# Split edge searches, a division moved to VectorE, and seven-product forms for layer 0's neighbour sums and two chunks of the second v projection

## The chip, the cores and the metric

One NeuronCore of a Trainium2 chip. The time is the device time of one execution of the whole kernel, in microseconds (us); a lower number is better. TensorE is also called PE (its weight loads PEld), VectorE DVE, ScalarE ACT, GpSimd POOL and SyncE SP. All arrays are f32.

## The reference

A graph network over N = 384 nodes and 12672 edges, in two blocks with a residual and a normalisation before each. First 16-head attention of width 1024 under a mask that is built from the edges; then a relational graph convolution of two layers (width 768, R = 6 relations, B = 4 bases).

```python
h = relu(layernorm(x))
q, k, v = h @ wq.T + bq, h @ wk.T + bk, h @ wv.T + bv
q2, k2, v2 = q @ wiq.T + biq, k @ wik.T + bik, v @ wiv.T + biv      # 16 heads of 64
mask[src, dst] = softplus(w)[type5 - 1]        # -inf elsewhere, the diagonal always set
x = x + (softmax(q2 k2' / 8 + mask) v2) @ wo.T + bo

h = relu(layernorm(x)); y = relu(h @ w_in + b_in)
for l in 0, 1:
    W[r] = sum_b comp[l, r, b] * basis[l, b]
    agg[dst] += (y @ W[r])[src] / count[r, dst]     # every edge, by its relation r
    y = batchnorm(relu(agg + y @ root[l] + bias[l]) + y)
x = x + layernorm(y @ w_out + b_out)
```

## The kernel before

Nodes lie in three chunks of P = 128 (NT = 3), features in chunks of 128 too (KD = 8 for 1024, KC = 6 for 768). The orders of PE, DVE, POOL and SP, and after q of ACT, are those in which the code calls them: each engine runs its instructions in that order, and a waiting one holds back all behind it.

**Seven products.** A product of two matrices cut in 2 x 2 blocks is made with seven block products instead of eight. Sums of blocks are formed on DVE ahead of it (`output_sums` of weights, `node_sum` of nodes, in attention; `weight_sums`, `last_sums`, `node_sums` in the convolution); `multiply` or `times` runs one block product; ACT copies results out of PSUM and DVE adds others to them. A bank (of eight in PSUM) is used again in the same part, so PE waits there for the copy or addition that reads it. In attention, q2, k, k2 and v are made so, in four parts each (`plan`, 16 parts), with `rest` as the product that one part leaves to the next.

**Edges.** `edge_steps` is a generator; `fill(1)` advances it by one step in each part. It finds, for every edge, whether others fall in the same cell. `find_cells(p)` loads a piece of keys (SP), shifts them (DVE), runs one search for the mask (`find(0, ...)`: one DVE operation per 128 edges, 9 or 12 in most pieces) and returns the second search, that for the counts. In pieces from step 3 on both are called in the same step. POOL then scatters with indirect DMAs: `put_mask` (L261) into four mask tables and `put_count` (L266) into two count tables `atab`. The last `fill(1000)` issues what is left: the remaining counts on POOL, and on DVE the operations that merge the four mask tables into `mask8` (L308 to L315).

**Second v projection.** `second_v(half, t, w)` makes 512 columns of v2 for node chunk t with 8 matmuls of 512. Four of them run after v, the other two between the first scores (`scores`, `exponents`, `normalise` of the softmax).

**Counts.** When the scatters are done, SP and POOL load the tables into A (one [128, 3, 384] slice for each relation; the second table is added by the DMA). `add_up(r)` sums the slice over its three chunks on POOL; `share(r)` sums that over partitions with one matmul (ps_cnt), takes the reciprocal on DVE and multiplies A[:, r] by it on POOL; then `mix(l, r, At, bs)` adds comp times A[:, r] into At[:, b] (ACT for r = 0, DVE for the others). A written plan, `between`, puts shares and mixes between PE's matmuls: its key is (layer, basis, chunk), where chunk 4 stands for the end of a basis and basis B for the root product.

**A layer.** For each of four bases, seven products and two chunk rows make H = y @ basis[b] (L846, L840); then y @ root (L880) into six banks `pr`; then the neighbour sums, H' At over bases and node chunks, into the same banks. In layer 0 that is `add_neighbours`, 72 matmuls of 384 columns (L897), features' banks one after the other, with the weight sums of layer 1's first basis put after the third; in layer 1 it is seven products over three pairs of feature chunks (L947), 126 matmuls of 192 columns, whose operands T1..T4 (from At) and feature sums (from H) DVE makes just before.

Of the kernel before, what the change touches and what calls it, by code (L numbers as in the profile page):

```python
# [51 lines left out]
def gnn_kernel(ctx: ExitStack, tc: tile.TileContext, out, x, edges, chunks, cols, rows, small,  # L52
# [120 lines left out]
    def edge_steps(ep, none, zero):  # L173
# [115 lines left out]
        for find_more in rest:  # L289
            find_more()  # L290
        for step in range(2, 18):
            yield
            for i in {5: (0,), 6: (1,), 7: (2, 3), 8: (4, 5)}.get(step, (step - 4,) if 10 <= step < 16 else ()):
                clear(i // R, i % R)
            if step in (3, 6, 8, 10, 12, 14, 16):
                find_cells(max(3, step // 2 + 1))()
            for p in {8: (3,), 9: (4,), 10: (5,), 11: (6,), 16: (7, 8), 17: (9,)}.get(step, ()):
                put_rounds(p)
# [31 lines left out]
    def add_up(r):  # L330
        sums[r] = late.tile([P, N], F32, tag="sum", name="sum", bufs=2)
        nc.gpsimd.tensor_tensor(sums[r], A[:, r, 0, :], A[:, r, 1, :], ALU.add)
        nc.gpsimd.tensor_tensor(sums[r], sums[r], A[:, r, 2, :], ALU.add)

    def share(r):

        ps = next_bank("ps_cnt", ring[1:])
        nc.tensor.matmul(ps[:, :N], ones, sums[r], start=True, stop=True)
        rn = late.tile([P, N], F32, tag="rn", name="rn", bufs=2)
        nc.vector.tensor_scalar(rn, ps[:, :N], 1.0, None, ALU.max)  # L340
        nc.vector.reciprocal(rn, rn)  # L341
        nc.gpsimd.tensor_tensor(A[:, r], A[:, r], rn[:, None, :].to_broadcast([P, NT, N]), ALU.mult)  # L342
        if r + 2 < R:
            add_up(r + 2)


    with ExitStack() as inner:
# [68 lines left out]
        with tc.tile_pool(name="edge", bufs=1, side="right") as ep:  # L416
# [101 lines left out]
            q2, k2, v = made["q2"], made["k2"], made["v"]  # L518
            v2 = ap.tile([P, NT, D], F32, tag="T", name="v2", bufs=4)

            def second_v(half, t, w):
                ps = next_bank("ps_v2", (4, 5, 6, 7))
                for k in range(KD):
                    nc.tensor.matmul(ps, v[:, k, t * P:(t + 1) * P], w[k // 4][:, k % 4, :],  # L524
                                     start=(k == 0), stop=(k == KD - 1))
                return lambda: nc.scalar.copy(v2[:, t, half * 512:(half + 1) * 512], ps)

            for half in range(2):
                w = [wload(wiv[half, j], "w_v2") for j in range(2)]
                for t in range(NT - 2 * half):  # L530
                    second_v(half, t, w)()
# [87 lines left out]
        for f in (0, 2):  # L619
            scores(f)  # L620
            scores(f + 1)
            put_v = second_v(1, f // 2 + 1, w)
# [9 lines left out]
        for g in range(STEPS + 1):  # L632
# [14 lines left out]
            if f + 2 == STEPS:  # L647
# [9 lines left out]
                for r in range(R):  # L657
# [3 lines left out]
                    if 0 < r < 3:  # L661
# [104 lines left out]
    with tc.tile_pool(name="conv", bufs=1) as cp:  # L766
# [41 lines left out]
        def mixes(l, r, *bs):  # L808
            return lambda: mix(l, r, At, bs)

        between = {(0, 1, 1): shares(0), (0, 1, 2): shares(1),
                   (0, 2, 0): lambda: (mix(0, 0, At), share(2)), (0, 2, 1): mixes(0, 1, 0, 1), (0, 2, 2): mixes(0, 1, 2, 3),
                   (0, 2, 4): shares(3),
                   (0, 3, 0): mixes(0, 2, 0, 1), (0, 3, 1): lambda: (mix(0, 2, At, (2, 3)), share(4)),
                   (0, 3, 2): mixes(0, 3, 0, 1), (0, 3, 4): shares(5),
                   (0, 4, 0): mixes(0, 4, 0, 1), (0, 4, 1): mixes(0, 5, 0, 1), (0, 4, 2): mixes(0, 3, 2, 3),
                   (0, 4, 3): mixes(0, 4, 2, 3), (0, 4, 4): mixes(0, 5, 2, 3),
# [10 lines left out]
        for l in range(L):  # L828
# [49 lines left out]
            for k in range(KC):  # L878
                for o in range(KC):
                    nc.tensor.matmul(pr[o], w[k // 2][:, k % 2, o * P:(o + 1) * P], XT[:, k, :], start=(k == 0),  # L880
                                     stop=(k == KC - 1 and l == L - 1))
                if k == 0:
                    rest()
                go_between(l, B, k)
            if l + 1 < L:
                w = load_basis(l + 1, 0)
            else:

                room = late.tile([P, R * NT * N], F32, tag="A", name="room")
                rowsB = room[:, :3 * D].rearrange("p (j d) -> p j d", j=3)  # L890
                for j, r in enumerate((R_BOUT, R_LNG, R_LNB)):
                    nc.scalar.dma_start(rowsB[:, j, :], rows[r:r + 1, :].to_broadcast([P, D]))

            def add_neighbours(o, bs):
                for b in bs:
                    for n in range(NT):
                        nc.tensor.matmul(pr[o], H_[:, b, n, o * P:(o + 1) * P], At[:, b, n, :],  # L897
                                         start=False, stop=(b == B - 1 and n == NT - 1))
# [21 lines left out]
            def begin(o, func=AF.Identity):  # L920

                c = l * KC + o
                nc.scalar.activation(XN[:, o, :], pr[o], func, bias=cols_sb[:, CB + c:CB + c + 1])

            if l + 1 < L:
                for o in range(KC):
                    add_neighbours(o, (0, 1))
                for o in range(KC):
                    add_neighbours(o, (2, 3))
                    begin(o, AF.Relu)  # L930
                    normalise_layer(*measure(o))
                    if o == 2:
                        T = weight_sums(w)
            else:


                def h(o, i):

                    return H_.rearrange("p b n d -> p (b n) d")[:, i * 6:i * 6 + 6, o * P:(o + 1) * P]

                def q(i, j):

                    return At.rearrange("p b n d -> p (b n) d")[:, i * 6:i * 6 + 6, j * HN:(j + 1) * HN]

                def times(ps, x, y, start=False, stop=True):
                    for c in range(6):
                        nc.tensor.matmul(ps, x[:, c], y[:, c], start=start and c == 0, stop=stop and c == 5,  # L947
                                         skip_group_check=True)

                room2 = keep.tile([P, KD * N], F32, tag="hT", name="room2")  # L950
                T1, T2 = [room2[:, i * 1152:(i + 1) * 1152].rearrange("p (c d) -> p c d", c=6) for i in range(2)]
                T4 = keep.tile([P, 6, HN], F32, tag="mask8", name="T4")
                nc.vector.tensor_tensor(T1, q(0, 1), q(0, 0), ALU.subtract)
                nc.vector.tensor_tensor(T2, q(1, 1), T1, ALU.subtract)
                T3 = q(0, 1)
                nc.vector.tensor_tensor(T3, q(1, 1), q(0, 1), ALU.subtract)
                nc.vector.tensor_tensor(T4, q(1, 0), T2, ALU.subtract)
                spaces = [room2[:, 2304:]] + [room[:, 3 * D + i * 768:3 * D + (i + 1) * 768] for i in range(5)]
                spaces = [v.rearrange("p (c o) -> p c o", c=6) for v in spaces]

                def feature_sums(p):

                    s0, s1, s3 = spaces[p % 2 * 3:][:3]
                    o0, o1 = 2 * p, 2 * p + 1
                    S.append((s0, s1, h(o1, 0), s3))
                    for dst, x, y, op in ((s0, h(o1, 0), h(o1, 1), ALU.add), (s1, s0, h(o0, 0), ALU.subtract),
                                          (h(o1, 0), h(o0, 0), h(o1, 0), ALU.subtract),
                                          (s3, h(o0, 1), s1, ALU.subtract)):
                        nc.vector.tensor_tensor(dst, x, y, op)
                        yield  # L970

                S = []
                for _ in feature_sums(0):
                    pass
                pairs = KC // 2

                def take(o, j, ps):
                    dst = XN[:, o, j * HN:(j + 1) * HN]
                    nc.vector.tensor_tensor(dst, dst, ps, ALU.add)

                def rectify(o):
                    nc.scalar.activation(XN[:, o, :], XN[:, o, :], AF.Relu)
                    return o

                def first_of(p):
                    pa = next_bank("ps_c", range(8))[:, :HN]
                    times(pa, h(2 * p, 0), q(0, 0), True)
                    return pa

                pa = first_of(0)  # L990
                for p in range(pairs):
                    times(pr[2 * p][:, :HN], h(2 * p, 1), q(1, 0))
                for o in range(KC):
                    begin(o)
                take(0, 0, pa)
                ready = None
                for p in range(pairs):
                    last = p == pairs - 1
                    sums = iter(()) if last else feature_sums(p + 1)
                    o0, o1 = 2 * p, 2 * p + 1  # L1000
                    pc = next_bank("ps_c")[:, :HN]
                    times(pc, S[p][0], T1, True)
                    take(o1, 1, pc)
                    if ready:
                        normalise_layer(*ready)
                    next(sums, None)
                    times(pa, S[p][1], T2)
                    take(o0, 1, pa)
                    next(sums, None)
                    times(pc, S[p][3], q(1, 1))  # L1010
                    take(o0, 1, pc)
                    ready = measure(rectify(o0))
                    if last:
# [118 lines left out]
```

## Time and profile before

| what | value |
|---|---|
| three runs | 744.85 us median (740.45 to 747.54) |
| the profiled execution's own time | 735.77 us |
| its span, first to last instruction | 734.0 us |
| PE, PEld busy | 713.5, 496.8 us |
| DVE, POOL, ACT busy | 472.9, 323.3, 147.2 us |
| PE clock granted, mean | 0.996 |

The profile is of one execution. Busy time is what an engine's instructions took; the PE column counts two records for each f32 matmul. A row of a group reads: line, engine, operation, output <- inputs, shape, count | busy us, mean ns of one | idle time before them and what ended most of it. In a timeline row, the idle time before an instruction stands in brackets with its releaser. A releaser is inferred; where several were waited for it is the last one seen.

### The profile page before, as it was taken

Reading aid. Unit: us, or ns where it says so; the run is one execution under the profiler, and the core shown is the slowest. Engines: PE = TensorE matmul, PEld = TensorE weight load, DVE = VectorE, ACT = ScalarE, POOL = GpSimd, SP = SyncE. Lnnn points to the kernel's source line nnn. Section 1 sums busy time; section 2 is a strip of 40 time slices with the busy share of each in tenths; the row PEclk is TensorE's granted clock in tenths of the full one; section 3 lists DMA queues with packets and bytes.
Section 4 is the critical chain, followed back from the end, with each engine's and each line's share of the span. In section 5 each row is a group of like instructions: output and inputs, shape, how many; then the busy total and the mean of one; then the engine's idle time right before and its main releaser. Section 6 shows DMA issues by size and latency. Waiting matters only on the chain.

```text
span 734.0 us, 8299 instructions
## 1 busy us (share of the span) xinstructions
PE 713.5 (97%) x3024; PEld 496.8 (68%) x3024; DVE 472.9 (64%) x1228; ACT 147.2 (20%) x338; POOL 323.3 (44%) x242
## 2 busy tenths in 40 slices
PE   8999989999999999999999999899999999999995
PEld 8759989999964444445995555555555555579943
DVE  6895897877504499625424779990187676506756
ACT  3201111111111477510131131100013111001100
POOL 1456777788886788587784454310000000030000
PEclk9999999999999999999999999999999999999999
DMA  7797766743447322623527953321003123700001
GB/s 296 261 346 231 221 182 209 212 148 115 116 119 240 59 1 2 215 0 47 127 2 169 312 163 129 129 83 46 0 1 107 66 85 129 271 29 1 1 29 57
DMA packets 40533, 90.96 MB, mean 124 GB/s; under 512 B 19644, under 2 KB 27680, under 8 KB 36270
## 3 DMA queue, kind: packets, MB, share of 16 engines
q1 hardware_dynamic: 18478, 79.62, 30.9%
q0 software_dynamic: 21008, 8.42, 10.4%
q10 hardware_dynamic: 1008, 2.41, 0.9%
q8 instruction: 23, 0.38, 0.2%
q14 instruction: 16, 0.13, 0.1%
HBM read 79.27 MB, written 11.16 MB: 123 GB/s over the span
## 4 chain that ended last, share of the span: by engine, by line
PE 86%; DVE 11%; ACT 1%; issue 1%; DMA 1%; DVEq 0%; ACTq 0%
PE ps_g L846 13%; PE ps_g L840 10%; PE ps_c L897 6%; PE ps_c L880 6%; PE ps_q L395 6%; PE ps_v L524 6%; PE ps_k L377 6%; PE ps_c L947 6%; PE ps_v L377 5%; PE ps_y L615 5%; PE ps_f L1054 4%; DVE same L250 3%; PE ps_q L377 3%; PE ps_x L377 3%; PE ps_o L608 2%; PE ps_s L563 2%
## 5 line engine op out<-in xcount | busy, mean ns | idle before, releaser
L266 POOL DMA_INDIRECT atab<-count,at x99 | 160.0, 1616 | 50.6 <-DMA atab<-count,at 26.2
L261 POOL DMA_INDIRECT mtab<-m_val,at x99 | 104.1, 1052 | 57.0 <-issue 24.4
L1041 POOL TENSOR_TENSOR x_sb<-x_sb,room 128x1024 f32<-128x1024 f32 x3 | 7.0, 2347 | 158.1 <-DMA room<-in_rows 158.1
L326 DVE SCALAR_TENSOR_TENSOR At<-A,small_sb,At 128x1152 f32<-128x1152 f32 x40 | 62.9, 1635 | 0.0
L840 PE MATMUL ps_g<-T,S 128*128 128x384 f32 x144 | 49.1, 486 | 0.0
L846 PE MATMUL ps_g<-w_c,XT 128*128 128x384 f32 x144 | 48.0, 487 | 0.0
L846 PE MATMUL ps_g<-w_c,XN 128*128 128x384 f32 x144 | 47.6, 486 | 0.0
L897 PE MATMUL ps_c<-At,H 128*128 128x384 f32 x144 | 46.6, 486 | 0.0
L395 PE MATMUL ps_q<-hT,w_q 128*128 128x384 f32 (+1 forms) x160 | 41.8, 422 | 1.4 <-ACT hT L90 1.4
L524 PE MATMUL ps_v<-w_v,v 128*128 128x512 f32 x96 | 41.9, 594 | 0.0
L840 PEld LDWEIGHTS ps_g<-T,S 128*128 128x128 f32 x144 | 27.4, 190 | 19.1
L897 PEld LDWEIGHTS ps_c<-At,H 128*128 128x128 f32 x144 | 27.4, 190 | 19.1
L846 PEld LDWEIGHTS ps_g<-w_c,XN 128*128 128x128 f32 x144 | 27.4, 190 | 19.1
L846 PEld LDWEIGHTS ps_g<-w_c,XT 128*128 128x128 f32 x144 | 27.2, 190 | 19.2 <-DVE H L861 0.6
L395 PEld LDWEIGHTS ps_q<-hT,w_q 128*128 128x128 f32 x160 | 28.5, 190 | 14.1 <-ACT hT L90 1.7
L377 PE MATMUL ps_k<-T,S 128*128 128x192 f32 x192 | 35.8, 330 | 0.0
L615 PE MATMUL ps_y<-w_o,attT 128*128 128x512 f32 x80 | 35.0, 595 | 0.0
L576 DVE CUSTOM_DVE_ANT_0 s<-ps_s,mask 128x384 f32<-128x384 f32 x48 | 24.5, 548 | 15.4 <-PE ps_s L563 15.4
L342 POOL TENSOR_TENSOR A<-A,rn 128x1152 f32<-128x1152 f32 x6 | 19.4, 3236 | 31.7 <-DVE rn L341 31.7
L524 PEld LDWEIGHTS ps_v<-w_v,v 128*128 128x128 f32 x96 | 18.0, 190 | 22.6 <-issue 22.6
L377 PEld LDWEIGHTS ps_k<-T,S 128*128 128x128 f32 x192 | 32.7, 194 | 0.0
L1054 PE MATMUL ps_f<-w_out,XN 128*128 128x512 f32 (+1 forms) x84 | 31.1, 531 | 0.0
(250 smaller groups left out, 1316.6 us busy)
## 6 DMA issues: line engine op xcount, KB each, us to landing
w_c<-in_basis SPq DMA_DIRECT2D x24, 768.0 KB, 6.2
atab<-zero SPq DMA_DIRECT2D x12, 576.0 KB, 8.2
A<-atab POOLq DMA_DIRECT2D x10, 576.0 KB, 9.8
w_c<-in_root SPq DMA_DIRECT2D x6, 768.0 KB, 5.5
w_q<-in_wq SPq DMA_DIRECT2D x4, 1024.0 KB, 11.8
w_q<-in_wiq SPq DMA_DIRECT2D x4, 1024.0 KB, 10.1
w_k<-in_wk SPq DMA_DIRECT2D x4, 1024.0 KB, 7.0
w_k<-in_wik SPq DMA_DIRECT2D x4, 1024.0 KB, 6.2
```

The costliest lines, as they stand in the source:

```text
L261: nc.gpsimd.indirect_dma_start(mtab[c // PER][:, :], bass.IndirectOffsetOnAxis(at[:, 0, c:c + 1], 0), m_val[:, c:c + 1], None)
L266: nc.gpsimd.indirect_dma_start(atab[0 if i < 18 - DEALT else i % 2][:, :], bass.IndirectOffsetOnAxis(at[:, 1, c:c + 1], 0), count[:, 1, c: ...
L326: nc.vector.scalar_tensor_tensor(At[:, b], A[:, r], w, At[:, b], ALU.mult, ALU.add)
L377: nc.tensor.matmul(ps, a[:, k, :], b[:, k, :], start=start and k == 0, stop=(k == 3), skip_group_check=not start)
L395: nc.tensor.matmul(ps[o][:, c], wt_[:, k, o * P:(o + 1) * P], src[:, k, c], start=(k == 0 and c.start == 0), stop=(k == KD - 1 and c.stop ...
L524: nc.tensor.matmul(ps, v[:, k, t * P:(t + 1) * P], w[k // 4][:, k % 4, :], start=(k == 0), stop=(k == KD - 1))
L615: nc.tensor.matmul(ps, attT[:, k, t * P:(t + 1) * P], w_o[half][k // 4][:, k % 4, :], start=(k == 0), stop=(k == KD - 1))
L840: nc.tensor.matmul(ps, x[:, c], y(c), start=start and c == 0, stop=(c == 2), skip_group_check=not start)
L846: nc.tensor.matmul(ps, block(XT, n, i)[:, c], w[c][:, i, o * HC:(o + 1) * HC], start=(first and c == 0), stop=(c == 2 and (i == 1 or ps is ...
L880: nc.tensor.matmul(pr[o], w[k // 2][:, k % 2, o * P:(o + 1) * P], XT[:, k, :], start=(k == 0), stop=(k == KC - 1 and l == L - 1))
L897: nc.tensor.matmul(pr[o], H_[:, b, n, o * P:(o + 1) * P], At[:, b, n, :], start=False, stop=(b == B - 1 and n == NT - 1))
L1054: nc.tensor.matmul(p, XT[:, k, t * P:(t + 1) * P], w[k // 2][:, k % 2, c0:c1], start=(k == 0), stop=(k == KC - 1))
```

## The change

1. *Searches*: from step 3 on, the second search of a piece is called in the step after the first.
2. *Division*: `share` multiplies A[:, r] on DVE; four `sums` tiles instead of two, so that `add_up` of relations 0 to 3 is issued with A's transfers on POOL, and `share(r)` issues that of r + 4. The plan `between` of layer 0 is written anew.
3. *Second v projection*: chunks 0 and 1 are made in seven block products for each half; chunk 2 stays as it was and runs between the first scores.
4. *Layer 0's neighbour sums* take the form that layer 1's had. Its sums lie in other tiles, one of them of the weights' pool.

```diff
         for find_more in rest:
             find_more()
+        rest = []
         for step in range(2, 18):
             yield
+            if rest:
+                rest.pop()()
...
             if step in (3, 6, 8, 10, 12, 14, 16):
-                find_cells(max(3, step // 2 + 1))()
+                rest.append(find_cells(max(3, step // 2 + 1)))
...
-        sums[r] = late.tile([P, N], F32, tag="sum", name="sum", bufs=2)
+        sums[r] = late.tile([P, N], F32, tag="sum", name="sum", bufs=4)
...
-        nc.gpsimd.tensor_tensor(A[:, r], A[:, r], rn[:, None, :].to_broadcast([P, NT, N]), ALU.mult)
-        if r + 2 < R:
-            add_up(r + 2)
+        nc.vector.tensor_tensor(A[:, r], A[:, r], rn[:, None, :].to_broadcast([P, NT, N]), ALU.mult)
+        if r + 4 < R:
+            add_up(r + 4)
...
+            VS = [sum_tile(i).rearrange("p k n -> p (k n)")[:, :512].rearrange("p (k n) -> p k n", k=4)
+                  for i in (1, 2, 3, 4)]
+            for dst, a, b, op in ((VS[0], va(1, 0), va(1, 1), ALU.add), (VS[1], VS[0], va(0, 0), ALU.subtract),
+                                  (VS[2], va(0, 0), va(1, 0), ALU.subtract), (VS[3], va(0, 1), VS[1], ALU.subtract)):
+                nc.vector.tensor_tensor(dst, a, b, op)
...
+                for dst, a, b in ((T1, vb(half, 0, 1), vb(half, 0, 0)), (T2, vb(half, 1, 1), T1),
+                                  (T3, vb(half, 1, 1), vb(half, 0, 1)), (T4, vb(half, 1, 0), T2)):
+                    nc.vector.tensor_tensor(dst, a, b, ALU.subtract)
+                return T1, T2, T3, T4
...
+            VT = [output_weights(half) for half in range(2)]
+            def v_products(half):
+                pa, pb, pc = [ps[:, :256] for ps in vbanks[half]]
+                T1, T2, T3, T4 = VT[half]
+                multiply(pa, va(0, 0), vb(half, 0, 0), True)
+                nc.scalar.copy(v_out(half, 0, 0), pa)
+                yield
+                multiply(pb, va(0, 1), vb(half, 1, 0), True)
+                add_out(half, 0, 0, pb)
+                yield
+                multiply(pc, VS[0], T1, True)
+                nc.scalar.copy(v_out(half, 1, 1), pc)
+                yield
+                multiply(pa, VS[1], T2)
+                nc.scalar.copy(v_out(half, 0, 1), pa)
+                yield
+                multiply(pc, VS[3], vb(half, 1, 1))
+                add_out(half, 0, 1, pc)
+                yield
...
+                multiply(pd, va(1, 1), T4, True)
+                multiply(pa, VS[2], T3)
+                def last():
+                    nc.scalar.copy(v_out(half, 1, 0), pa)
+                    add_out(half, 1, 1, pa)
+                    add_out(half, 1, 0, pd)
+                yield last
+            first, second = v_products(0), v_products(1)
+            for products, n in ((first, 2), (second, 2), (first, 3)):
+                for _ in range(n):
+                    next(products)
+            next(first)()
+            for _ in range(3):
+                next(second)
+            next(second)()
             fill(1000)
...
-            put_v = second_v(1, f // 2 + 1, w)
+            put_v = second_v(f // 2)
...
-                    if 0 < r < 3:
+                    if 0 < r < 5:
                         add_up(r - 1)
...
-        between = {(0, 1, 1): shares(0), (0, 1, 2): shares(1),
-                   (0, 2, 0): lambda: (mix(0, 0, At), share(2)), (0, 2, 1): mixes(0, 1, 0, 1), (0, 2, 2): mixes(0, 1, 2, 3),
-                   (0, 2, 4): shares(3),
-                   (0, 3, 0): mixes(0, 2, 0, 1), (0, 3, 1): lambda: (mix(0, 2, At, (2, 3)), share(4)),
-                   (0, 3, 2): mixes(0, 3, 0, 1), (0, 3, 4): shares(5),
-                   (0, 4, 0): mixes(0, 4, 0, 1), (0, 4, 1): mixes(0, 5, 0, 1), (0, 4, 2): mixes(0, 3, 2, 3),
-                   (0, 4, 3): mixes(0, 4, 2, 3), (0, 4, 4): mixes(0, 5, 2, 3),
+        between = {(0, 1, 0): shares(0), (0, 1, 1): shares(1), (0, 1, 2): lambda: mix(0, 0, At),
+                   (0, 1, 4): mixes(0, 1, 0, 1), (0, 2, 0): shares(2), (0, 2, 2): shares(3),
+                   (0, 2, 4): mixes(0, 2, 0, 1), (0, 3, 0): shares(4), (0, 3, 1): shares(5),
+                   (0, 3, 4): lambda: [mix(0, r, At, (0, 1)) for r in (3, 4, 5)],
+                   **{(0, 4, r): mixes(0, r, 2, 3) for r in range(1, R)},
...
+            room2 = keep.tile([P, KD * N], F32, tag="hT", name="room2")
+            spaces = [room2[:, 2304:]]
             if l + 1 < L:
+                spaces += [v.rearrange("p i k o -> p (i k o)")[:, i * 768:(i + 1) * 768] for v, n in
+                           ((cp.tile([P, 4, 3, P], F32, tag="S", name="sums"), 2),
+                            (wpool.tile([P, 2, 6, P], F32, tag="w", name="sums"), 2)) for i in range(n)]
+                spaces.append(cp.tile([P, 3, HC], F32, tag="T4", name="sums").rearrange("p c d -> p (c d)")[:, :768])
                 w = load_basis(l + 1, 0)
...
-            if l + 1 < L:
-                for o in range(KC):
-                    add_neighbours(o, (0, 1))
-                for o in range(KC):
-                    add_neighbours(o, (2, 3))
-                    begin(o, AF.Relu)
-                    normalise_layer(*measure(o))
-                    if o == 2:
-                        T = weight_sums(w)
-            else:
...
             XT = XN
             if l + 1 < L:
                 S = node_sums(XT)
+                T = weight_sums(w)
```

## The prediction

> **What bounds the kernel now.** I read the page's busy shares, then TensorE's waits by releaser, then its instructions in order of time around each wait. Columns of a waits row: who waited for whom, total us, times, longest. Of a timeline row: start, us, engine, line, tile, shape, count, and what ended the idle time before it.
>
> ```profile
> PE 713.5 (97%) x3024; PEld 496.8 (68%) x3024; DVE 472.9 (64%) x1228; ACT 147.2 (20%) x338; POOL 323.3 (44%) x242
> ```
>
> ```profile
> PE ps_k L377 <- DVE k L502: 4.3, 3, 2.9
> PE ps_c L880 <- DVE H L853: 2.2, 1, 2.2
> PE ps_v L377 <- DVE v L502: 1.1, 1, 1.1
> ```
>
> ```profile
> 101.48 1.46 PE L377 MATMUL ps_k<-T,S 128*128 128x192 f32 x8
> 105.86 2.61 PE L377 MATMUL ps_k<-T,w_k 128*128 128x192 f32 x8 [2.92 <-DVE k L502]
> 108.26 2.14 PE L377 MATMUL ps_k<-T,S 128*128 128x192 f32 x8
> ```
>
> TensorE (PE) is busy 97% of 734.0 us: time goes only with PE work or PE waits. Nearly all waits are on VectorE (DVE), in two places: the searches (L250) and the end of layer 0's last basis.
>
> The chain that ended last, by time, prices the PE work (start, us, what; one f32 matmul leaves two records):
>
> ```profile
> 209.96 27.47 PE ps_v L524 x64
> 348.05 6.91 PE ps_y L687 x32
> 499.77 46.44 PE ps_c L897 x144
> 654.57 40.95 PE ps_c L947 x252
> ```
>
> So 512 columns cost 0.858 us, 256 cost 0.432, 384 cost 0.645 and 192 cost 0.325: width alone counts.
>
> **Split searches.** The 16 parts of q2, k, k2 and v are 7 products of 1.30 us each: 145.6 us. They stand between 55.55 and 209.96, 154.4 us: 8.8 lost. The waits are 5.7 of it (4.3, 1.1, and 0.3 in q2). The 2.92 wait costs more: its two next groups take 4.38 (105.86 to 110.24) instead of 2.60, and the clock over 103 to 112 was 0.81. In a searching part DVE has sums 2.5, key shift 0.95, two searches of 3.7 each, plus adds, against 9.1 us of PE. Split, the part has 7.1 plus adds and the next gets the other 3.7. Tightest is part 0 of q2: T sums end 58.82, S sums 61.35, search 65.05, and the add that frees the bank 65.6; PE wants it at 65.95. I take 8.5 gained. Ends: 5 (small waits come back) and 8.8.
>
> Here a rule is weighed. The Trainium skill, "TensorE: Matmul & The Clock Gate", Part 1 (What's actually happening), puts the drop to half rate after an idle window of some 3.4 us. The idle here is 3.08 (102.78 to 105.86), under a window, so read strictly it costs nothing beyond itself and the edit brings 7.0. The row shows 1.78 more: I take the row. For the new waits below, each under 2 us, the short waits' row holds (after 1.1 us of waiting at 183.70 the group took 0.1 more).
>
> **Second v projection.** Two chunks leave L524: 32 matmuls of 512 (27.47) become 7 products x 4 x 2 halves = 56 of 256, 24.2. Chunk 2 keeps 16 matmuls beside the scores, as before. Gain 3.3. DVE gets 4 sums of 512, 8 of 1024 and 8 adds out of PSUM: about 2.5 + 9.3 + 3. Count from the end of ps_v L377. v is whole at 0.5; the sums of half 0 end at 7.8, half 1 at 12.4; PE wants them from 6.9 (only T1, ready by 4.4) and 15.6: covered. The last add ends at 25.1. *Behind it in DVE's queue stand the mask operations* (L308 to L315), today at 224.1 to 232.6 in idle time. They take 8.5, so the mask is ready at 33.7. PE has done four scores and the 7.07 of second_v at 32.8 and wants banks 0 to 3 again; the exponents free them from 34.1 to 35.6. PE waits 1.7; with restart 1.8. Ends: 0 and 4. Net of this part: 1.5.
>
> **The relation table is the new limit.** Upstream gains make 8.5 + 1.5 = 10.0. But the table comes from POOL's scatters, which do not speed up:
>
> ```profile
> 385.05 1.55 POOL L266 DMA_INDIRECT atab<-count,at  x1 [0.30 <-issue]
> 392.67 1.36 POOL L658 DMA_DIRECT2D A<-atab  x1 [6.07 <-DVE T L795]
> ...
> 404.19 1.01 POOL L332 TENSOR_TENSOR sum<-A 128x384 f32<-128x384 f32 x1
> 405.28 1.60 POOL L333 TENSOR_TENSOR sum<-sum,A 128x384 f32<-128x384 f32 x1
> ```
>
> (I read the 6.07 as the landing of SP's A<-atab, issued at 388.11.) The first two sums stand at 401.1 and 406.9. The counts of relations 0 and 1 move one site earlier: on today's clock to 409.7 and 414.2. Ten us earlier, the second is wanted at 404.2. A scatter stretches beside a DVE operation with two SBUF inputs (2.36 at 200.29, inside L516's 1.22, against 1.55), and v's new sums are such: I add 1.0 to the chain, so sum 1 stands at 407.9. PE waits 3.7 over both; upstream keeps 6.3. Ends: chain 1.3 earlier (POOL's one wait on search results, gone) or 6 later. Upstream losses below 3.7 are thus free. On POOL two add_up pairs are put between the last A transfers. Sum 2 then stands near 414, sum 3 near 422, the last two by 434; they are wanted from 425 on, after the gain.
>
> **Division on DVE, mixes reordered.**
>
> ```profile
> L342 POOL TENSOR_TENSOR A<-A,rn 128x1152 f32<-128x1152 f32 x6 | 19.4, 3236 | 31.7 <-DVE rn L341 31.7
> ...
> 470.65 5.00 DVE L326 SCALAR_TENSOR_TENSOR At<-A,small_sb,At 128x1152 f32<-128x1152 f32 x2
> 555.15 5.39 DVE L326 SCALAR_TENSOR_TENSOR At<-A,small_sb,At 128x1152 f32<-128x1152 f32 x4
> 629.92 1.35 DVE L953 TENSOR_TENSOR room<-At 128x1152 f32<-128x1152 f32 x1
> ```
>
> A mix costs 2.5 beside POOL's division and 1.33 without POOL. The division itself is not in DVE's rows: nearest is L953, 1.35 (broadcast operand unseen; ends 1.3 and POOL's 3.24). The wait of 2.2 at 473.8 goes (PE stood 2.35, its group 0.2 slower): 2.6. Check with t = 0 at the first L846 (PE: basis 19.35 or 22.6 us each): a share is 0.58 + 2.6 + 1.35 = 4.5. DVE does sums 4.4, mixes 2.7, T4 1.5, two shares 9.0, adds 1.4 per basis: 19 in 22.6. ScalarE's first mix (4 x 1.2) stands ahead of its copies, ends as PE's next product runs: no wait. The reordered mixes give the cover back: last H add at 88, then 16 mixes, 21.3, to 109.
>
> **Neighbour sums of layer 0.** 72 matmuls of 384 (46.44) become 126 of 192, exactly L947's 40.95: gain 5.5. The rule that speaks against it: same page, Back-to-back issue gap, says that spacing is set by weight load and matmul both, so narrow matmuls pay more. The weight-load row has 190 ns, two per matmul: 0.38. Were they not hidden, 126 x 0.38 = 47.9, a loss of 1.4. But L947 ran at 0.325 on that very shape, so the loads overlap: 5.5. DVE adds 4 sums of At (5.3) and 4 feature sums (3.5) behind the mixes: At done 109, T1..T4 115, first S 116; PE wants At's second half at 114, S at 121. Cover 5. Per pair the code is the last layer's, where PE never waited. At the end DVE normalises 4.8 after PE's last product (700.3 against 695.5 today), then S 2.1, then weight sums 4.4; before, weight sums lay under L897. PE starts with layer 1's c = 0, which needs features 0 and 1 only, wants S at 11.6 (ready 6.9) and the last T1 at 12.9 (10.4): no wait, 1 to 2 us of cover. If gone: up to 3. SP's next basis loads go past one wpool tile lent to the sums, freed after pair 1, 12 us ahead of need.
>
> **Sum.** 6.3 + 2.6 + 5.5 = 14.4. The profiled span 734.0 becomes 719.6, its time 735.77 becomes 721.4. The median of the runs is 744.85, 9.1 above the profiled execution, so the forecast there is 744.85 - 14.4 = **730.4**.
>
> **Rivals.**
> 1. *Upstream is kept whole.* The chain comes earlier too, no wait for it or the mask: 744.85 - 8.8 - 3.3 - 2.6 - 5.5 = 724.7. For: 40 us of POOL's waits are DMA landings, not fixed. Against: 198 scatters of 1.05 and 1.62 with 0.3 between fill the rest. Chance 0.12.
> 2. *The table comes 6 later.* Sum 1 at 412.9, so upstream keeps 414.2 - 412.9 = 1.3: 744.85 - 1.3 - 8.1 = 735.4. For: scatters stretched beside v's sums, loads colliding with A's transfers. Against: the softmax's DVE work left scatters at 1.55. Chance 0.16.
> 3. *DVE becomes the bound of layer 0.* Division at 3.24 (+11.3 for six), mixes at 2.29 (first four today took 9.16; +19 for twenty), less 15 of cover: 15 late at the first S, 745. For: VectorE's share is over 9 tenths there now. Against: POOL has left but for twelve 1 us adds. Chance 0.06.
> 4. *Slower: the scatter chain takes over.* Each scatter at 2.36 instead of 1.55 delays sum 1 by 0.8, and from 406.9 on every us of it is the end's. Of the site's 7.3 (414.2 - 406.9) and the other parts' 8.1, together 15.4, nineteen stretched scatters leave nothing; thirty come 24 late, 744.85 + 24 - 15.4 = 753.5. Place: the scatters from 210 to 386. Against: the new DVE work there is 15 us, some 8 scatters. Chance 0.04.
>
> Forecast 0.62. A measurement of this kernel can tell about 1%, 7.4 us. Faster by over 1% (below 737.4): forecast, 1 and nearly all of 2, 0.87; within: 3 and the rest, 0.09; slower 0.04. The range reaches from rival 1, less most of the runs' spread (the lowest is 4.4 under the median), to rival 2 and as much of it above: 721 to 739.
>
> **What would show it.** Right: no wait on DVE in ps_q, ps_k, ps_v of over 0.5 and clock 1.00 there; ps_v2 24.2 us; a wait of about 1.7 at a score for the mask chain; waits of together 2 to 5 at ps_cnt, for POOL's sums; none at L880; layer 0's neighbour sums 41 us. Wrong: a gap of over 1 us at the first S product or at the start of layer 1; sum 1 after 414; search waits again over 3.

## The result, and the profile after

| kernel | median us | lowest to highest | runs | against the kernel before |
|---|---|---|---|---|
| before, first runs | 744.5 | 740.45 to 747.54 | 4 | |
| after, first runs | 731.18 | 729.67 to 733.46 | 4 | 0.9855 (0.9808 to 0.9901) |
| before, beside the experiments | 737.7, 737.94, 737.6 | 735.44 to 743.63 | 44, 39, 18 | |
| after again | 731.04 | 727.54 to 736.98 | 13 | 0.9912 (0.9887 to 0.9937) |

The changed kernel takes 731 us, as forecast (730.4). But the forecast was 14.4 us under a median of 744.85, and 101 later runs of the kernel before, on three chips, have medians near 737.7. The first four runs of before lay high; beside 18 of its runs the changed kernel is 0.9% faster (6.6 us), not the 1.5% of the first comparison. Why the first four lay high is not known. The two profiled spans agree with the smaller gain: 734.0 and 727.9. The number came out right by luck: a gain taken 8 us too large was subtracted from a base 7 us too high. The question is therefore where 8 us of gain went.

The profile page, first lines of after (busy us, share of the span, instructions):

```profile
span 727.9 us, 8691 instructions
...
PE 704.6 (97%) x3180; PEld 518.6 (71%) x3180; DVE 502.2 (69%) x1289; ACT 150.8 (21%) x348; POOL 301.6 (41%) x236
```

TensorE has 8.9 us less work than before (713.5) and is still busy 97%. Its waits have other names now (who waited for whom, total us, times, longest):

```profile
PE ps_cnt L341 <- POOL sum L336: 6.4, 1, 6.4
PE ps_s L641 <- DVE top L654: 1.9, 1, 1.9
PE ps_k L380 <- ACT k L497: 1.7, 2, 1.1
```

The waits on the searches and on H are gone. In their place stand a wait for the relation table's first sum, one at the scores for the mask, and two for ScalarE's copies of k. In the chain that ended last (start, us, what), the parts that answer to L687 and L897 of before:

```profile
340.95 6.91 PE ps_y L765 x32
499.14 40.95 PE ps_c L1014 x252
```

The neighbour sums of layer 0 now equal layer 1's to the hundredth; what was not touched kept its price. The second v projection on TensorE's timeline, its first products and the first score after it:

```profile
203.28 7.07 PE L380 MATMUL ps_v<-w_v,v 128*128 128x256 f32 x32
227.55 1.56 PE L641 MATMUL ps_s<-k,q 64*128 64x384 f32 x8
```

That is 24.3 us from mark to mark, where before had 27.6 (209.8 to 237.36). GpSimd in order of time (start, us, engine, line, tile; what ended its idle time), the counterpart of the table's rows:

```profile
388.64 1.55 POOL L266 DMA_INDIRECT atab<-count,at  x1 [0.32 <-DMA atab<-count,at]
396.12 1.36 POOL L736 DMA_DIRECT2D A<-atab  x1 [5.93 <-DVE H L937]
396.93 1.38 POOL L738 DMA_DIRECT2D A<-atab  x1
...
407.03 0.99 POOL L335 TENSOR_TENSOR sum<-A 128x384 f32<-128x384 f32 x1 [6.62 <-DMA A<-atab]
408.10 0.99 POOL L336 TENSOR_TENSOR sum<-sum,A 128x384 f32<-128x384 f32 x1
```

The last scatter is 3.6 later than before (385.05), and the accumulating transfer of relation 0, started at 396.12, has landed only at 407: 10.9 us, where before it took 6.4 (392.67 to 399.05). What TensorE does about it (L341 is the count):

```profile
409.14 1.65 PE L341 MATMUL ps_cnt<-sum,ones 128*128 128x384 f32 x2 [6.39 <-POOL sum L336]
410.58 6.00 PE L922 MATMUL ps_g<-w_c,XT 128*128 128x384 f32 x12
416.42 0.81 PE L341 MATMUL ps_cnt<-sum,ones 128*128 128x384 f32 x2
417.06 4.03 PE L922 MATMUL ps_g<-w_c,XT 128*128 128x384 f32 x12
```

After 6.39 of waiting the first count takes 1.65 instead of 0.81 and twelve records of L922 take 6.00 instead of 4.03: 2.8 us more. The granted clock was 0.50 from 407.7 to 414.5. A late sum costs its wait and then a stretch at half clock, called the restart below.

**Stage by stage.** Each number is the stretch between two marks on TensorE's timeline: first second-v product, first score, first L922, first neighbour sum, first product of layer 1 (209.8, 237.36, 384.52, 499.61, 546.04 in the first profile of before). Change from before to after, us:

| stage | prediction | first profiles | second profiles |
|---|---|---|---|
| to the second v (searches) | -8.5 | -6.5 | -8.9 |
| second v, before the scores | -3.3 | -3.3 | -3.3 |
| scores to the first basis (mask) | +1.8 | +2.7 | +5.8 |
| bases and root (counts, division) | +1.1 | +6.5 | +7.6 |
| neighbour sums of layer 0 | -5.5 | -5.5 | -5.5 |
| layer 1 and the end | 0 | 0 | 0 |
| sum | -14.4 | -6.1 | -4.3 |

The rows of work are right. The sum falls short by 8.3 and 10.1 us. The rows of the mask and of the counts hold 6.3 of it in the first profiles and 10.5 in the second; the other 2.0 of the first is in the searches.

### The profile page after: what moved, and what is told of

The parts are those of the page before. It is cut to its first block, busy times and chain, and to the rows that moved or that the text cites. A ratio compares the mean times of both kernels' runs of the same rounds, so it can differ in the third digit from the quotient of the medians.

```text
span 727.9 us, 8691 instructions
## 1 busy us (share of the span) xinstructions
PE 704.6 (97%) x3180; PEld 518.6 (71%) x3180; DVE 502.2 (69%) x1289; ACT 150.8 (21%) x348; POOL 301.6 (41%) x236
## 3 DMA queue, kind: packets, MB, share of 16 engines
q1 hardware_dynamic: 18478, 79.62, 30.9%
q0 software_dynamic: 21008, 8.42, 10.1%
## 4 chain that ended last, share of the span: by engine, by line
PE 91%; DVE 5%; DMA 2%; ACT 1%; issue 1%; POOL 0%; DVEq 0%; ACTq 0%
PE ps_g L922 12%; PE ps_c L1014 11%; PE ps_k L380 10%; PE ps_g L916 10%; PE ps_v L380 8%; PE ps_c L956 6%; PE ps_q L398 6%; PE ps_q L380 5%; PE ps_y L693 5%; PE ps_f L1120 4%; PE ps_x L380 3%; PE ps_o L686 2%; PE ps_s L641 2%; PE ps_pT L675 2%; DMA A<-atab 1%; PE ps_v L565 1%
## 5 line engine op out<-in xcount | busy, mean ns | idle before, releaser
L329 DVE SCALAR_TENSOR_TENSOR At<-A,small_sb,At 128x1152 f32<-128x1152 f32 x40 | 53.7, 1413 | 0.0
L922 PE MATMUL ps_g<-w_c,XT 128*128 128x384 f32 x144 | 49.9, 501 | 0.0
L922 PE MATMUL ps_g<-w_c,XN 128*128 128x384 f32 x144 | 47.6, 486 | 0.0
L922 PEld LDWEIGHTS ps_g<-w_c,XT 128*128 128x128 f32 x144 | 28.4, 198 | 20.2 <-issue 2.4
L922 PEld LDWEIGHTS ps_g<-w_c,XN 128*128 128x128 f32 x144 | 27.3, 190 | 18.8
L1014 PE MATMUL ps_c<-At,H 128*128 128x192 f32 x216 | 36.4, 326 | 0.0
L1044 DVE TENSOR_TENSOR XN<-XN,ps_c 128x192 f32<-128x192 f32 x38 | 12.6, 349 | 34.4 <-ACT XN L1000 19.7
L1014 PEld LDWEIGHTS ps_c<-At,H 128*128 128x128 f32 x216 | 35.4, 190 | 0.5
L250 DVE SCALAR_TENSOR_TENSOR same<-keys,key,weigh 128x128 f32<-128x128 int32 x99 | 28.0, 345 | 1.1 <-DVE same L250 1.1
L693 PEld LDWEIGHTS ps_y<-w_o,attT 128*128 128x128 f32 x80 | 15.0, 190 | 18.9 <-issue 18.9
L250 DVE SCALAR_TENSOR_TENSOR same<-cells,own,later 128x128 f32<-128x128 int32 x99 | 27.9, 348 | 0.4
```

Of the source, the lines that this page charges most:

```text
L250: nc.vector.scalar_tensor_tensor(same, row[:, n, :], mine[:, c:c + 1], times, ALU.is_equal, ALU.mult, accum_out=count[:, i, c:c + 1])
L329: nc.vector.scalar_tensor_tensor(At[:, b], A[:, r], w, At[:, b], ALU.mult, ALU.add)
L693: nc.tensor.matmul(ps, attT[:, k, t * P:(t + 1) * P], w_o[half][k // 4][:, k % 4, :], start=(k == 0), stop=(k == KD - 1))
L922: nc.tensor.matmul(ps, block(XT, n, i)[:, c], w[c][:, i, o * HC:(o + 1) * HC], start=(first and c == 0), stop=(c == 2 and (i == 1 or ps is ...
```

## The experiments

All but the last two kernels are before or after, unchanged or with one edit.

**1. Each part alone, on the kernel before.** The edits are the parts of the diff shown above.

```diff
 searches_only:   + rest.append(find_cells(...)), called one step later
 v_only:          + v_products for chunks 0 and 1, second_v(f // 2) beside the scores
 division_only:   + nc.vector.tensor_tensor(A[:, r], ...), four sums, the new `between`
 neighbours_only: + layer 1's form of the neighbour sums in layer 0
```

> The kernel before with the split searches alone. Theory (the searches gave 6.6 us in the changed kernel, and a table that lands late takes gains from upstream back): the end of the first v products moves from 209.96 to about 203.4, no TensorE wait on VectorE in ps_q, ps_k, ps_v. The counts are taken one site later than in the changed kernel, so they are wanted at about 403 and 407.6, against sums at 401.1 and 406.9 in the profile before: the gain is kept, 6 to 7 us (ratio 0.991). Rival (basis loads that now start 6.6 earlier collide with the transfers of A): sums 5 or more later, TensorE waits there, and 2 to 4 us of the gain are left (ratio 0.996). Prediction's own price for the searches: 8.5 (ratio 0.9886).

> The kernel before with the seven block products for v alone. Theory (3.3 us less TensorE work, 2.6 us given back at the scores where the mask chain is late): net 0 to 1.5 us faster, ratio 0.998 to 1.000, ps_v 24.2 us, one wait of about 2 at a score on VectorE. Rival (the mask wait is only late because the searches made TensorE early): no wait, ratio 0.9955.

> The kernel before with the division on VectorE, the counts one site earlier and the mixes in the new order, alone. Theory (the wait at the last basis goes; counts are wanted at 405 and 409.7, the sums stand at 401 and 407): 2.6 us faster, ratio 0.9965, no wait at ps_cnt. Rival (moving the counts a site earlier is what makes the table late, with or without the rest): a wait of 2 to 5 us at ps_cnt and a ratio of 1.000 to 1.003.

> The kernel before with layer 0's neighbour sums in seven block products alone; the old mixes and the division on GpSimd stay. Theory (TensorE work falls from 46.4 to 41.0 and VectorE keeps up): 5.5 us faster, ratio 0.9926. Rival (with the old order of mixes the sums of At come late): a wait on VectorE at the first S or T product and 2 to 4 us faster.

| alone | median us (before 737.7) | ratio | to second v, from the first scatter | scores to basis | bases and root | last scatter, from the first | A's first landing |
|---|---|---|---|---|---|---|---|
| before | | | 183.5 | 147.2 | 115.1 | 358.8 | 6.4 |
| searches | 738.41 | 0.9997 (0.9977 to 1.0017) | 174.7 | 147.2 | 125.4 | 362.0 | 9.9 |
| v | 741.55 | 1.0053 (1.0035 to 1.0071) | 181.9 | 151.7 | 122.3 | 363.2 | 6.3 |
| division | 736.55 | 0.9979 (0.9961 to 0.9997) | 183.8 | 147.2 | 113.1 | 358.4 | 6.4 |
| neighbours | 732.59 | 0.9931 (0.9904 to 0.9958) | 183.7 | 147.2 | 115.6 | 358.3 | 6.4 |

(Times in us, two columns counted from the first scatter, which starts anywhere from 26.2 to 29.2; that of v_only was the latest, so its 181.9 shows no gain.) The searches alone bring their 8.8, and in the profile lose all of it and 1.5 more in the bases: gain upstream, none at the end, on 14 runs against 44. My theory that later counts would save it fell; the rival named the right mechanism and still left too much. v alone makes the kernel slower, by 3.9 us; its profile is of its slowest execution (746.45), so its stages are longer than usual. There TensorE waits 2.0 at the scores, 1.7 at ps_cnt and 4.7 for VectorE's H. The neighbour sums do what the working said, the division somewhat less: 2.0 in the profile and 1.2 in the medians, of 2.6. GpSimd in searches_only, the same stretch as above:

```profile
389.70 1.55 POOL L266 DMA_INDIRECT atab<-count,at  x1 [0.30 <-issue]
397.31 1.36 POOL L661 DMA_DIRECT2D A<-atab  x1 [6.07 <-DVE H L866]
...
407.25 0.99 POOL L335 TENSOR_TENSOR sum<-A 128x384 f32<-128x384 f32 x1 [5.70 <-DMA A<-atab]
```

One edit far upstream moves both the last scatter and the landing. TensorE then waits 3.0 at ps_cnt and 4.0 in the bases for VectorE's H, and its groups behind these two waits take 4.9 longer, at half clock from 408.6 to 415.4 and from 452.9 to 456.4. Before had only the 2.2 at L880 there, of which 0.6 is left.

**2. The kernel before once more.**

> The kernel before, unchanged, with a second profile. Its timed runs took 740.5 to 747.5, its one profiled execution 735.8. Theory (what differs between executions is the TensorE clock after the waits on the searches, and scatters): a span 5 to 10 us longer than 734.0 shows its extra time between 55 and 210, with clock under 1.00 there. Rival (the extra time lies at the relation table, where TensorE waits for the sums): the first v products end near 210 as before, and a wait appears at ps_cnt.

Its 20 timed runs have a median of 739.05 (733.89 to 743.66), ratio 1.0013 (0.9995 to 1.0030). The profiled execution has a span of 734.1, with every mark within 0.3 us of the first. So it was not one of the longer executions, and its profile tests neither theory. But every timed run has its mean granted clock on record. Of the 101 runs of before, the 25 slowest (740.7 on average) lose 7.4 us to lowered clock, counted as span x (1 - clock); the 25 fastest (735.9) lose 3.2. That is 4.2 of the 4.7 us between them, so the clock is what mostly differs; where in the execution stays open. What the profile settles: it repeats, and lies 2 us under the median of the 101 and not 9.

**3. Counts later.**

```diff
-        between = {(0, 1, 0): shares(0), (0, 1, 1): shares(1), (0, 1, 2): lambda: mix(0, 0, At),
-                   (0, 1, 4): mixes(0, 1, 0, 1), (0, 2, 0): shares(2), (0, 2, 2): shares(3),
+        between = {(0, 1, 2): shares(0), (0, 1, 4): lambda: (share(1), mix(0, 0, At)),
+                   (0, 2, 0): shares(2), (0, 2, 1): mixes(0, 1, 0, 1), (0, 2, 2): shares(3),
```

> The changed kernel with the first two counts taken later, after (0,1,2) and (0,1,4), and the mixes that need them moved behind. Theory (the table is what binds: 6.4 us of waiting and 2.9 us of slow clock after it): no wait at ps_cnt, clock 1.00 over 400 to 420, and 8 to 9 us faster than the changed kernel (about 722). Rival (VectorE then has the shares and mixes closer together and is late in basis 2 or 3): a wait on VectorE in ps_g or ps_c and at most 4 us gained.

726.77 us, 0.9870 (0.9811 to 0.9929). TensorE's waits in the bases are then down to one:

```profile
PE ps_g L922 <- DVE H L937: 2.7, 1, 2.7
```

and the count comes without waiting, at full clock, though the first sum was ready 4 us later than in after:

```profile
406.08 7.90 PE L922 MATMUL ps_g<-w_c,XT 128*128 128x384 f32 x24
413.82 0.81 PE L341 MATMUL ps_cnt<-sum,ones 128*128 128x384 f32 x2
```

Bases and root take 115.2 instead of 121.5: 6.3 us in this profile, 4.3 in the medians, between the theory (8 to 9) and the rival (at most 4). There are only 4 runs, and their interval overlaps that of after again (0.9887 to 0.9937); the same edit brings 5.0 in experiment 7. This shows that the count sites are what the late table acts through. The 2.7 on VectorE is the rival's part.

**4. SP's basis loads held back** until relation 0 has landed.

```diff
                 for r in range(R):
                     nc.gpsimd.dma_start(A[:, r], tabs[1][r], accum_op=ALU.add)
...
+                    if r == 1:
+                        nc.sync.dma_start(keys_d[0:1, 0:1].bitcast(F32), A[0:1, 0, 0, 0:1])
```

> The changed kernel with SP's basis loads held back behind a four-byte transfer that reads A of relation 0, so that they start when its table has landed. Theory (A's transfers took 10.8 us instead of about 6 because basis loads share the DMA engines): landing falls to 6 or 7, the wait at ps_cnt from 6.4 to 2, and 4 to 6 us are gained unless the held loads are then late for basis 1 and 2. Rival (the accumulating transfer is slow by itself): landing stays at 10 to 11, the wait at ps_cnt stays 6 or more, and late loads can only cost.

```profile
395.53 1.37 POOL L736 DMA_DIRECT2D A<-atab  x1 [6.09 <-DMA A<-atab]
396.33 1.38 POOL L738 DMA_DIRECT2D A<-atab  x1
397.13 1.88 POOL L736 DMA_DIRECT2D A<-atab  x1
...
401.79 0.99 POOL L335 TENSOR_TENSOR sum<-A 128x384 f32<-128x384 f32 x1 [1.98 <-DMA A<-atab]
...
410.64 1.72 POOL L335 TENSOR_TENSOR sum<-A 128x384 f32<-128x384 f32 x1 [2.67 <-DMA A<-atab]
```

Relation 0 lands in 6.3 us again (395.53 to 401.79): the 10.9 was a collision with the basis loads. SP issued these at 393.75 in after and at 400.84 in before:

```profile
393.75 1.62 SPq L80 DMA_DIRECT2D w_c<-in_basis  x3
```

They wait until a weights' tile is free (8.7 us for TensorE's L840 in before, 8.0 for VectorE's sum L873 in after), and a basis that is done early starts them early. Held to 402.08 they hit relation 1 instead, which started at 397.13 and has landed at 410.64: the waits at the counts become 2.06 and 5.00, another 2.5 for ScalarE's H appears, and the kernel takes 735.36 us, 0.9968 (0.9949 to 0.9987), slower than after. The cause is shown; this is no cure.

**5. After without the new second v.**

```diff
-            first, second = v_products(0), v_products(1)
+            for half in range(2):
+                w = [wload(wiv[half, j], "w_v2") for j in range(2)]
+                for t in range(NT - 2 * half):
+                    second_v(half, t, w)()
```

> The changed kernel with the second v projection undone. Theory (v's sums delay the scatters by 2 to 3 us, and its net gain upstream is wiped out by the wait for the table): the last scatter lands 2 to 3 us earlier, the wait at ps_cnt shrinks by 3 to 4, and the time is 0 to 3 us below the changed kernel. Rival (the v products are worth their 3.3 less 2.6): 0.7 us slower than the changed kernel with the same end of the scatter chain.

731.01 us, 0.9916 (0.9896 to 0.9937), as after again (0.9912). The part is worth nothing that 4 runs can show in this kernel, in line with the theory's end, but not by its way: the last scatter comes 362.5 us after the first, in after 362.4. v's sums do not delay the table here; the searches alone already have 362.0. What v gains, the mask takes: without it the stretch from the first score to the bases is 147.6, with no wait at the scores, against 149.9 and 152.8 in the two profiles of after.

**6. After again.**

> The changed kernel, unchanged, beside many runs of the kernel before. Theory (the kernel before had a slow draw of four runs at 744.5; its median over 83 later runs is 737.8, and the two profiled spans differ by 6.1): 731 against 738, ratio 0.991. Rival (the first comparison was right): ratio 0.985 or 0.986.

The ratio is the theory's. Its profile shows no wait for ScalarE's copies in ps_k (1.7 in the first one), and the searches' full 8.9. But the same waits elsewhere were dearer:

```profile
PE ps_cnt L341 <- POOL sum L336: 7.6, 1, 7.6
PE ps_s L641 <- DVE top L654: 2.0, 1, 2.0
```

TensorE after the second of these, in the first profile of after:

```profile
238.07 2.34 PE L641 MATMUL ps_s<-k,q 64*128 64x384 f32 x8 [1.89 <-DVE top L654]
240.34 7.13 PE L565 MATMUL ps_v<-w_v,v 128*128 128x512 f32 x16
247.41 1.56 PE L641 MATMUL ps_s<-k,q 64*128 64x384 f32 x8
```

and in the second:

```profile
235.73 3.40 PE L641 MATMUL ps_s<-k,q 64*128 64x384 f32 x8 [1.99 <-DVE top L654]
239.06 8.94 PE L565 MATMUL ps_v<-w_v,v 128*128 128x512 f32 x16
247.94 1.56 PE L641 MATMUL ps_s<-k,q 64*128 64x384 f32 x8
```

The wait is the same; what follows it costs 0.8 us in one and 3.7 in the other. In the first the granted clock stayed at 1.00, in the second it was 0.50 from 235.9 to 242.7.

**7. The mask tables' transfers on SP**, ahead of the loads of wo; then with late counts; then with the mask's operations ahead of v's last adds too.

```diff
-                    nc.gpsimd.dma_start(v, tab[:MCELLS, :]...)
+                    nc.sync.dma_start(v, tab[:MCELLS, :]...)
...
-            next(second)()
-            fill(1000)
+            put_last = next(second)
+            fill(1000)
+            put_last()
```

> The changed kernel with the four transfers of the mask tables issued by SP, where they stand ahead of the loads of wo, instead of by GpSimd between two scatters. Theory (TensorE that is early releases the loads of wo into the mask tables' transfers, and the scatters behind them wait 4 to 9 us; the table is then what the end waits for): the wait of a scatter near 230 goes, GpSimd is spared 3.4 us of issuing, the last scatter starts at 385 or earlier instead of 388.6, the wait at ps_cnt falls from 6.4 to 0 to 3, and 4 to 8 us are gained (725). Rival (scatters wait for each other whatever the loads do): last scatter at 388 or later, no gain.

> The same with the first two counts also taken later, as in late_shares. Theory (the table binds): no wait at ps_cnt, the whole gain upstream is kept, 719 to 723. Rival (with the table out of the way VectorE is what is late in the bases): waits on VectorE in ps_g of 3 us or more, 725 or above.

> The same again, with the mask's operations issued ahead of the last two adds of v. Theory (the wait of 1.9 to 4.0 at the scores is the mask chain standing behind those adds): the wait at ps_s goes or falls under 1, 1 to 3 us below mask_on_sp_late. Rival (the mask tables land late, so that the adds now wait for them, and banks with them): no gain, or a wait in ps_v2 in its place.

| kernel | median us | ratio (after again, beside the same runs of before: 0.9912) |
|---|---|---|
| mask_on_sp | 730.52 | 0.9899 (0.9874 to 0.9924) |
| mask_on_sp_late | 725.49 | 0.9845 (0.9808 to 0.9882) |
| mask_on_sp_late_first | 729.13 | 0.9893 (0.9867 to 0.9919) |

The first theory fell. A scatter beside the mask tables waits as long as in after (4.32 at 230.81):

```profile
222.18 1.55 POOL L266 DMA_INDIRECT atab<-count,at  x1 [1.15 <-DMA atab<-count,at]
228.22 1.99 POOL L266 DMA_INDIRECT atab<-count,at  x1 [4.50 <-DMA atab<-count,at]
```

and the last one starts at 391.22, so the loads of wo are not what makes the scatters late. With late counts the kernel is again some 5 us faster, 725.49: with late_shares the fastest of this study, and faster than both kernels. That is short of its theory (719 to 723); VectorE's wait in the bases is 2.1, less than its rival asked. The third lost 3.6 of that, the rival's case: VectorE then waits for the mask tables with v's adds behind it, and the 1.9 at the scores becomes

```profile
PE ps_v L565 <- DVE v L570: 7.8, 1, 7.8
```

## Why the prediction was right in its number and wrong in its working

- **Searches, -8.5 (ends 5, 8.8): right.** 8.8 alone, 8.9 in the second profile. The first profile of after shows 6.5 because ScalarE's copy L497 twice started at the end of the next product and not of its own; the second does not have it, and no run tells why.
- **Clock after waits: mis-sized.** The step "for the new waits below, each under 2 us, the short waits' row holds" put 0.1 on the mask wait. The wait itself was 1.9 as priced (1.7), what followed it 0.8 to 4.05. The rule weighed there, in the Trainium skill's "TensorE: Matmul & The Clock Gate", Part 1 (What's actually happening), would make it zero, as no wait under 3.4 us fills an idle window. Row and rule both fall short. That page also says that the window runs freely, so that the number of slow matmuls at a kernel's start differs from run to run; the two rows above, in mid-kernel, differ likewise. The timed runs show the size: by span x (1 - clock), after again loses 8.8 us (median of 13) and before, beside it, 4.0 (median of 18). Up to 4.8 of the missing 8 us are thus lowered clock.
- **Second v, 3.3 less work: right; net 1.5: wrong.** From v to the first basis the change was -0.6 in one profile and +2.5 in the other; most of the difference is the clock after the mask wait. Undone, it changes nothing at the end.
- **The table is the new limit: right; its size is the step that failed.** The sum said sum 1 at 407.9, 3.7 us of waiting, upstream keeps 6.3. Sum 1 stood at 413.5. Of its 5.6, 2.6 is scatters (3.6 later, 1.0 allowed), and the rest the landing, which I took over from before at some 6 us, though the working itself moves SP's basis loads earlier onto it. The wait came at relation 0's sum: the working leaves it at 402.1 (401.1 and the 1.0), it stood at 409.1, by 2.6 of scatters and 4.5 of landing (10.9 for 6.4). Wait and restart cost 9.2, against 3.7. "Upstream losses below 3.7 are thus free" holds in a wider sense: of the searches' 8.8 alone nothing is left.
- **Rival 2 is what happened.** It named the collision and had sum 1 at 412.9. Against the base that holds (737.7) it gives 737.7 - 9.4 = 728.3, the forecast 723.3; measured 731.0. What both lack is the clock after the waits (2.8 at the count alone).
- **Division and mixes, -2.6: right, rather less** (2.0 in the profile alone, 1.2 in the medians; the division 1.36 as taken from L953, a mix 1.41 on average instead of 1.64):

```profile
L345 DVE TENSOR_TENSOR A<-A,rn 128x1152 f32<-128x1152 f32 x6 | 8.2, 1359 | 0.5
```

- **Neighbour sums, -5.5: right.** 40.95, no wait at the first S or at layer 1's start; alone 5.1 in the medians.
- **The base.** The step from the profile to the median added 9.1 us of three runs to a profile that was 9 us faster. Those 9 us held in no later set: the median there is 2 us above the profile.

Open: why the scatters end 3 to 7 us later, counted from the first, in every kernel with split searches or the new v. By the 132nd scatter the four profiles with neither stand at 219.0 to 219.7 us after the first, the ten others at 221.1 to 228.2. Where just ahead of it the time goes is not shown: the twelve scatters up to it, beside the mask tables, took 30.9 us in one profile of before and 34.4 in the other, 35.5 in after and 36.8 with split searches alone. With the mask tables' transfers on SP the 132nd stands at 222.4 (224.9 in after) and the last at 363.4 (362.4): what was saved was lost again later.

## What to carry to other kernels

An engine that gets faster also frees its buffers sooner, so loads start sooner: list the transfers that the new schedule will start early and look for what they now overlap, as A's landing of 6.4 became 10.9. Price a new TensorE wait as wait plus what follows it, 0.8 to 4 us for a wait of 2 here, and give it as a range: the same wait was followed by no half clock, or by 3.4 or 6.8 us of it. When a chain that does not speed up (here the scatters) feeds a fixed site, move the site with it before making anything upstream faster. And three runs that disagree with the profile by 9 us are no base: difference the profiles, and let the base be measured.

## What the runs showed of the hardware

- The same wait of 1.9 to 2.0 us at the scores was followed by extra TensorE time of 0.8, 3.7, 2.1, 4.05, 2.1 and 2.4 us in six executions (after, after again, mask_on_sp, mask_on_sp_late, hold_loads, v_only). In the first of them the granted clock over 240 to 255 us was 1.00:

```profile
240.00:255.00 15.00, 15.00 (x60) 6.93 (x58) 10.44 (x39) 8.57 (x25) 9.89 (x8) 1.00 0.36 76
```

  in after again it was 0.91, in mask_on_sp_late 0.82:

```profile
240.00:255.00 15.00, 15.00 (x56) 7.15 (x56) 7.59 (x30) 6.13 (x18) 10.51 (x8) 0.91 0.37 70
```

```profile
240.00:255.00 15.00, 15.00 (x45) 6.75 (x44) 7.38 (x29) 6.23 (x19) 11.50 (x8) 0.82 0.38 70
```

  (Columns: stretch, us, busy us of PE, PEld, DVE, ACT, POOL with their instructions, clock, DMA share, GB/s.)
- These means come from stretches at half clock. The one in after again lies at 235.9 to 242.7:

```profile
236.00:242.00 6.00, 6.00 (x12) 2.99 (x12) 5.51 (x23) 5.19 (x17) 3.99 (x3) 0.50 0.47 131
```

  Behind that wait at the scores it is 6.8 us long in after again and mask_on_sp_late, 3.4 in mask_on_sp, hold_loads and v_only, and absent in after. Half of it, 3.4 or 1.7, is the extra time but for 0.2 to 0.8. That rest is not clock: without_v, with no wait, has 0.5 of it (2.03 for the second eight score records, 1.56 for the first) at clock 1.00. In the 14 profiles every half-clock stretch from 20 to 700 us is 3.4, 6.8 or 10.2 us long.
- An accumulating transfer of GpSimd's queue (relation 0's) lands in 6.3 to 6.4 us in the six profiles where no loads of weights by SP start just ahead of it, and in 9.8 to 12.0 in the eight where they start 0.8 to 3.9 us ahead. In v_only they start 2.1 us behind it, and it lands in 6.3.
